# GpSimd instead of VectorE multiplies the one-hot rows of c with the three weight parts

## The chip, the cores and the metric

The kernel runs on one core of a Trainium2 chip. The core has a matrix engine (PE, TensorE), a vector engine (DVE, VectorE), an activation engine (ACT, ScalarE), a general engine (POOL, GpSimd) and a queue that issues transfers (SP, SyncE). Each engine works through its own list of instructions in order; semaphores make one engine wait for another. The metric is the device time of one execution in microseconds (us), taken as the median of several runs.

## The reference

The input is x of shape 2 x 4096 x 256, in f32. First comes a token mixer made of cumulative sums over phases, gates and a projection; it is added to x after a layer norm. Its result goes through a layer norm into a mixture of single-vector experts, and this is the part that the change is in:

```python
s1 = jnp.einsum('bshd,nd->bshn', q1, K1)      # 8 heads, 64 keys on either side
s2 = jnp.einsum('bshd,nd->bshn', q2, K2)
v1, i1 = jax.lax.top_k(s1, TOPK)              # TOPK = 10
v2, i2 = jax.lax.top_k(s2, TOPK)
all_scores = (v1[..., :, None] + v2[..., None, :]).reshape(B, S, N_HEADS, TOPK * TOPK)
all_indices = (i1[..., :, None] * N_SQRT + i2[..., None, :]).reshape(B, S, N_HEADS, TOPK * TOPK)
vals, best = jax.lax.top_k(all_scores, TOPK)
expert_idx = jnp.take_along_axis(all_indices, best, axis=-1)
scores = jax.nn.softmax(vals, axis=-1)
h = jnp.einsum('bsd,bshkd->bshk', x, W_down[expert_idx])
h = jax.nn.gelu(h, approximate=False) * scores
out = jnp.einsum('bshk,bshkd->bsd', h, W_up[expert_idx])
```

Every token picks 8 x 10 = 80 experts. Their index is i1 * 64 + i2, so only the first 4096 of the 16384 experts can be picked.

## The kernel before

The tokens are worked through in 32 blocks of 256 (16 stretches of the sequence, two batch rows each). A block passes through these stages:

- `attention` is the token mixer; it makes `xt`, `x2T` (the normed input of the experts, transposed) and the queries.
- `routes` and `route` find the 80 experts of each token. This is long work on VectorE in small instructions (MAX8, FIND_INDEX8, MATCH_REPLACE8), then one-hot sums in the tile `hot`, then the softmax `sm`. GpSimd splits `sm` into three bf16 parts which together carry the f32 value (four instructions for each half block: two casts, two subtractions, into `pk` and `rest`). TensorE transposes them, and ScalarE copies them out as `row` and `rows`: then a partition is one of the 80 picks, and the free axis is the token.
- `hidden` multiplies the block with the down vectors of all 4096 experts (weights `wd`), and ScalarE applies gelu. The result `A` has expert j (128 of them) on the partitions, and c (32) and the tokens on the free axes. Expert number = j * 32 + c.
- `weigh` (lines 935 to 989) multiplies `A` with the router's weights. For each token TensorE makes a 128 x 32 matrix of weights, as the product of a one-hot matrix over j and a one-hot matrix over c that is multiplied with the weight. The inner function `build(t0)` makes these for 32 tokens at once: `hj`, eight comparisons of 128 x 512 on VectorE; `hc`, one comparison of 128 x 1024; and `hw`, the product of `hc` with the three weight parts, 128 x 3072 in bf16 (lines 959 to 964). Then for each token TensorE loads `hj` as weights and streams the three parts of `hw` into `ps_s`, 16 tokens to a PSUM tile. VectorE multiplies each such tile into `A`.
- `outputs` multiplies `A` with the up vectors (weights `wu`), norms, adds `xt` and stores.

`weigh` runs twice for each block, and `build` four times in each: 32 x 2 x 4 = 256 builds. `build` for the next 32 tokens is called ahead of the matrix products of the current ones. The tiles `hj`, `hc` and `hw` have two buffers each, `ps_s` has two, `row` and `rows` have three.

No engine call is issued where it is written. The class `Flow` records each call as a node with its dependencies. `plan` then orders all nodes by a list schedule: it gives each call a cost (`cost`, lines 166 to 196), keeps the time at which each engine is free, and lets each engine take the ready node with the lowest number. The number is the place at which the node was recorded; `together` interleaves three streams for that (experts of this block, routes of the next, attention of the one after it). `emit` writes the order out, with semaphore waits. So nearly all instructions carry line 404 in the profile, and are told apart by their tiles; the bare weight loads carry line 403, and the matrix products that use them line 401. The cost that `plan` takes for a call depends on the engine:

```python
            elif op in ("tensor_tensor", "tensor_mul", "tensor_add", "tensor_sub") and small:
                speed = 2
            return n / speed / 0.96 + 68, n / speed / 0.96 + 160
        ...
        return n * 2.4 + 200, n * 2.4 + 400          # gpsimd
```

A call that goes to another engine therefore changes the order in which all engines do their work, and not only the place of that one call.

Of the kernel before, what the change touches and what calls it, by code (L numbers as in the profile page):

```python
# [415 lines left out]
def layer_kernel(  # L416
# [9 lines left out]
    fl = Flow(nc, tc, ctx)  # L426
# [508 lines left out]
    def weigh(A, rows, before):  # L935

        row, rows = rows
        xj = fl.tile([P, 16, P], BF16, "xj")  # L940
        fl.vector.tensor_copy(xj[:, 0, :], row)
        for s in (8, 4, 2, 1):
            v = xj.rearrange("r (a b s) t -> r a b s t", b=2, s=s)
            fl.vector.tensor_scalar(v[:, :, 1, 0, :], v[:, :, 0, 0, :], 8.0 * s, None, ALU.subtract)

        yield 3

        def build(t0):
            hj = fl.tile([P, JE, TS], BF16, "hj")
            for i in range(8):  # L950
                fl.vector.tensor_scalar(hj.rearrange("r (m j) t -> r m j t", j=8)[:, :, i, :],
                                        xj[:, :, t0 : t0 + TS], float(i), None, ALU.is_equal)
            hc = fl.tile([P, TS, EC], BF16, "hc")
            fl.vector.tensor_tensor(
                hc.rearrange("r t (a u) -> r t a u", u=RUN),
                cols.rearrange("r (a u) -> r a u", u=RUN).unsqueeze(1).to_broadcast([P, TS, EC // RUN, RUN]),
                rows[:, t0 // TS, 0].unsqueeze(2).to_broadcast([P, TS, EC // RUN, RUN]), ALU.is_equal,
            )
            hw = fl.tile([P, 3, TS, EC], BF16, "hw")
            fl.vector.tensor_mul(  # L960
                hw.rearrange("r n t (a u) -> r n t a u", u=RUN),
                hc.rearrange("r t (a u) -> r t a u", u=RUN).unsqueeze(1).to_broadcast([P, 3, TS, EC // RUN, RUN]),
                rows[:, t0 // TS, 1:4].unsqueeze(3).to_broadcast([P, 3, TS, EC // RUN, RUN]),
            )
            return hj, hw

        ready = build(0)
        yield 3
        for t0 in range(0, P, TS):
            hj, hw = ready  # L970
            if t0 + TS < P:
                ready = build(t0 + TS)
                yield 3
            for g in range(0, TS, TG):
                ps = fl.tile([P, TG, EC], F32, "ps_s")
                for t in range(0, TG, TU):
                    with fl.group():
                        for i in range(t, t + TU):
                            w = hj[:, :, g + i]
                            fl.tensor.ld(ps[:, i, :], w)  # L980
                            for n in range(3):
                                fl.tensor.mm(ps[:, i, :], w, hw[:, n, g + i, :], start=n == 0, stop=n == 2)
                    next(before, None)
                a = A[:, :, t0 + g : t0 + g + TG]
                fl.vector.tensor_mul(a, ps.rearrange("p t c -> p c t"), a)
                yield 1
        for _ in before:
            pass
        yield 1
# [90 lines left out]
```

## Time and profile before

| | |
|---|---|
| median of 3 runs | 4083.58 us (4077.91 to 4088.07) |
| the profiled execution's own time | 4087.09 us |
| span of the profiled execution | 4085.3 us |
| mean granted clock of TensorE | 0.929 |
| busy: PE, DVE, ACT, POOL | 94%, 91%, 45%, 4% |
| instructions on POOL | 264, of which 256 are the splits of the softmax |
| `hw` products on DVE | 256, mean 1742 ns, 446.0 us in all |

A row of instructions gives the line, the engine, the operation, the tiles as out<-in, the shape and type of out and in, the count after the x, the time in which at least one of them was busy, the mean duration of one in ns, and the idle time of the engine just ahead of them with what ended it. The table of stretches gives for each stretch the microseconds in which each engine was busy, with the number of instructions that began in it. The timeline gives the start, the duration, the engine and the instruction. Consecutive instructions of DVE overlap in these records by some 80 ns: the record of one ends after the next one's has begun.

### The profile page before, as it was taken

How to read it: one execution, taken by the hardware profiler on the slowest of the kernel's cores; microseconds unless marked ns; L12 is line 12 of the kernel's file. 1: busy time of each engine (PE TensorE's matmuls, PEld its weight loads, DVE VectorE, ACT ScalarE, POOL GpSimd, SP SyncE). 2: the span in 40 equal slices, each digit the busy share in tenths (PEclk: the TensorE clock that was granted, in tenths of full speed). 3: DMA queues.
4: the chain of work that ended last, by engine and by line, in shares of the span. 5: the costliest groups of instructions: out<-in, count | busy, mean ns of one | idle time of the engine just before them, and what ended most of it. 6: DMA issues, size and time to landing. Idle time of an engine off the chain costs nothing.

```text
span 4085.3 us, 79868 instructions
## 1 busy us (share of the span) xinstructions
PE 3834.6 (94%) x36870; PEld 3300.2 (81%) x20486; DVE 3735.9 (91%) x17525; ACT 1837.9 (45%) x3251; POOL 153.9 (4%) x264
## 2 busy tenths in 40 slices
PE   3499999999999999999999999999999999999998
PEld 2388888888888888888888888888888888888887
DVE  3879999999999999999999999999999999999986
ACT  3344544444544444544444544444544444544431
POOL 0000000000000000000000000000000000000000
PEclk8699999999999999999999999999999999999989
DMA  5023333223333233333233333233333233333233
GB/s 205 29 93 120 106 115 123 90 96 127 101 116 125 89 100 124 106 115 123 91 96 127 100 117 125 89 100 124 98 122 122 90 98 126 103 115 125 86 108 121
DMA packets 145151, 447.83 MB, mean 110 GB/s; under 512 B 17777, under 2 KB 44146, under 8 KB 143730
## 3 DMA queue, kind: packets, MB, share of 16 engines
q1 hardware_dynamic: 139392, 440.46, 33.2%
q8 instruction: 225, 3.69, 0.4%
q10 hardware_dynamic: 5362, 2.28, 0.2%
q14 instruction: 172, 1.41, 0.1%
HBM read 425.90 MB, written 16.78 MB: 108 GB/s over the span
## 4 chain that ended last, share of the span: by engine, by line
PE 66%; DVE 31%; ACT 2%; ACTq 1%; issue 1%; DMA 0%; POOL 0%; POOLq 0%; SPq 0%
PE ps_mm L404 35%; PE ps_s L401 16%; PE ps_acc L404 12%; DVE hj L404 6%; DVE hw L404 4%; DVE hot L404 4%; PE ps_sc L404 3%; DVE ph L404 2%; DVE A L404 2%; DVE st L404 1%; DVE iu L404 1%; DVE hc L404 1%; DVE bl L404 1%; DVE v L404 1%; ACT rows L404 1%; DVE bu L404 1%
## 5 line engine op out<-in xcount | busy, mean ns | idle before, releaser
L404 PE MATMUL ps_mm<-x2T,wd 128*128 128x256 f32 x4096 | 1115.9, 423 | 44.2 <-ACT A L404 25.8
L403 PEld LDWEIGHTS <-hj 128*128 128x128 bf16 x8192 | 963.9, 141 | 103.2 <-DVE hw L404 29.0
L404 PEld LDWEIGHTS ps_mm<-x2T,wd 128*128 128x128 f32 x4096 | 854.0, 213 | 214.0 <-issue 81.9
L401 PE MATMUL ps_s<-hw,hj 128*128 128x32 bf16 x24576 | 994.9, 189 | 31.5 <-DVE hj L404 13.8
L404 PE MATMUL ps_acc<-wu,A 128*128 128x256 f32 x4096 | 1006.6, 393 | 6.9 <-DVE o L404 4.2
L404 PEld LDWEIGHTS ps_acc<-wu,A 128*128 128x128 f32 x4096 | 792.4, 197 | 123.5 <-DVE o L404 10.2
L404 ACT ACT_TABLE_LOAD x658 | 844.2, 1283 | 38.8 <-issue 26.0
L404 ACT ACTIVATE A<-ps_mm 128x256 f32<-128x256 f32 x1024 | 349.5, 383 | 976.3 <-PE ps_mm L404 961.3
L404 DVE TENSOR_SCALAR hj<-xj 128x512 bf16<-128x512 bf16 x2048 | 512.0, 302 | 0.0
L404 DVE TENSOR_TENSOR hw<-hc,rows 128x3072 bf16<-128x3072 bf16 x256 | 446.0, 1742 | 0.0
L404 DVE TENSOR_TENSOR A<-ps_s,A 128x512 f32<-128x512 f32 x512 | 346.7, 680 | 102.3 <-PE ps_s L401 62.4
L404 DVE FIND_INDEX8 iu<-v,s 128x8 uint32<-128x64 f32 x2048 | 428.1, 217 | 0.0
L404 DVE MAX8 v<-s 128x8 f32<-128x64 f32 x2048 | 374.3, 210 | 15.9 <-ACT s L404 15.9
L404 ACT ACTIVATE sm<-sm 128x80 f32<-128x80 f32 x64 | 17.3, 270 | 706.7 <-DVE sm L404 706.6
L404 DVE MATCH_REPLACE8 s<-v,s 128x64 f32<-128x64 f32 x1024 | 210.5, 208 | 0.0
L404 POOL CAST pk<-sm 128x80 bf16<-128x80 f32 x64 | 35.6, 556 | 3830.3 <-DVE sm L404 3830.3
L404 DVE TENSOR_TENSOR hc<-cols,rows 128x1024 bf16<-128x1024 bf16 x256 | 171.1, 678 | 0.0
L404 DVE MATCH_VALUE_LOAD iu<-v,s 128x8 f32 x2048 | 149.3, 73 | 0.0
L404 DVE RECIPROCAL rs<-rs 128x2 f32<-128x2 f32 (+1 forms) x160 | 22.3, 154 | 136.5 <-ACT rs L404 136.5
L404 PE MATMUL ps_mm<-x2T,wq 128*128 128x256 f32 x512 | 125.2, 388 | 1.0 <-ACT qT L404 0.6
L404 PE MATMUL ps_sc<-kbd,qT 128*128 128x256 f32 x512 | 124.8, 386 | 0.2 <-ACT qT L404 0.2
L404 PE MATMUL ps_mm<-xT,wg 128*128 128x256 f32 x512 | 122.3, 386 | 0.3 <-ACT tmp L404 0.3
(161 smaller groups left out, 4159.7 us busy)
## 6 DMA issues: line engine op xcount, KB each, us to landing
wu<-wu_d SPq DMA_DIRECT2D x512, 512.0 KB, 4.2
wd<-wd_d SPq DMA_DIRECT2D x256, 512.0 KB, 3.5
xt<-in_attn_x_dram SPq DMA_DIRECT2D x32, 256.0 KB, 2.9
A<-in_table_dram SPq DMA_DIRECT2D x8, 1024.0 KB, 7.2
out_dram<-o SPq DMA_DIRECT2D x64, 128.0 KB, 3.1
ph<-in_attn_pos_phases_dram SPq DMA_DIRECT2D x16, 256.0 KB, 3.9
wu_d<-A SPq DMA_DIRECT2D x8, 512.0 KB, 5.2
wd_d<-wd SPq DMA_DIRECT2D x8, 512.0 KB, 3.3
```

Of the source, the lines that this page charges most:

```text
L401: return engine.add_instruction(ins)
L403: return engine.ldweights(args[1], is_transpose=kw.get("is_transpose"), tile_position=(0, 0))
L404: return getattr(engine, op)(*args, **kw)
```

## The change

The product `hw` is issued on GpSimd; operands, shapes, types and buffers stay as they are.

```diff
             hw = fl.tile([P, 3, TS, EC], BF16, "hw")
-            fl.vector.tensor_mul(
+            fl.gpsimd.tensor_mul(
                 hw.rearrange("r n t (a u) -> r n t a u", u=RUN),
                 hc.rearrange("r t (a u) -> r t a u", u=RUN).unsqueeze(1).to_broadcast([P, 3, TS, EC // RUN, RUN]),
                 rows[:, t0 // TS, 1:4].unsqueeze(3).to_broadcast([P, 3, TS, EC // RUN, RUN]),
             )
```

## The prediction

> **What bounds the kernel now.** I read the page's first part, the chain of waits and the groups, and then a table of stretches over one block.
>
> ```profile
> PE 3834.6 (94%) x36870; PEld 3300.2 (81%) x20486; DVE 3735.9 (91%) x17525; ACT 1837.9 (45%) x3251; POOL 153.9 (4%) x264
> ...
> PE 66%; DVE 31%; ACT 2%; ACTq 1%; issue 1%; DMA 0%; POOL 0%; POOLq 0%; SPq 0%
> ...
> L404 DVE TENSOR_TENSOR hw<-hc,rows 128x3072 bf16<-128x3072 bf16 x256 | 446.0, 1742 | 0.0
> ```
>
> Two engines are nearly full, PE and DVE. The chain runs through PE for two thirds and through DVE for one third. POOL is all but idle. The moved product is 446.0 of DVE's 3735.9 us, so taken alone the change frees 12% of an engine that carries a third of the chain. In the stretches (span; busy us of PE, PEld, DVE, ACT, POOL with counts; clock; DMA share; GB/s) there are two kinds:
>
> ```profile
> 1931.00:2004.00 73.00, 70.07 (x868) 61.90 (x419) 70.98 (x310) 34.81 (x57) 2.47 (x4) 0.95 0.30 96
> 2004.00:2054.00 50.00, 48.32 (x285) 40.02 (x221) 46.65 (x241) 23.70 (x48) 2.27 (x4) 0.93 0.39 128
> ```
>
> All eight `hw` of a block start in the 73 us kind (the stretch has 8 of them, 13.61 us); the 50 us kind has none. PE and DVE are above 93% in both. So nothing waits idly for DVE time to come free, and nothing on DVE may get longer without the span getting longer.
>
> **What the profile says of POOL beside DVE.** POOL's own rows, by form:
>
> ```profile
> L404 POOL TENSOR_TENSOR rest<-sm,pk 128x80 f32<-128x80 f32 x64 | 31.6, 494 | 5.1
> L453 POOL IOTA iota<- 128x108 bf16 x1 | 0.3, 345 | 0.0
> masks.py:197 POOL MEMSET ident<- 128x128 f32 x1 | 0.2, 205 | 0.3 <-POOLq L1068 0.3
> L451 POOL IOTA cols<- 128x32 bf16 x1 | 0.2, 163 | 0.0
> ```
>
> And the places in the timeline where POOL's short instructions meet DVE's:
>
> ```profile
> 187.33 0.44 POOL L404 TENSOR_TENSOR rest<-sm,pk 128x80 f32<-128x80 f32 x1
> 187.45 0.38 DVE L404 TENSOR_TENSOR hot<-hot 128x80 uint16<-128x80 uint16 x1
> ...
> 1929.26 0.65 POOL L404 CAST pk<-rest 128x80 bf16<-128x80 f32 x1
> ...
> 1929.42 0.54 DVE L404 CAST pk<-ej 128x160 bf16<-128x160 uint16 x1
> ...
> 1998.10 0.19 DVE L404 CAST pk<-ej 128x160 bf16<-128x160 uint16 x1
> ...
> 1999.47 0.72 POOL L404 CAST pk<-rest 128x80 bf16<-128x80 f32 x1
> ...
> 1999.68 0.65 DVE L404 TENSOR_SCALAR hj<-xj 128x512 bf16<-128x512 bf16 x1
> ...
> 3962.28 0.68 POOL L404 TENSOR_TENSOR pk<-rest,pk 128x80 bf16<-128x80 f32 x1
> ...
> 3962.46 0.88 DVE L404 TENSOR_TENSOR hc<-cols,rows 128x1024 bf16<-128x1024 bf16 x1
> ```
>
> The same CAST takes 0.19 us alone and 0.54 us where it starts inside a POOL instruction: POOL's ends at 1929.91, the CAST's at 1929.96. An `hj` (median 282 ns) takes 0.65 us and ends at 2000.33, 0.15 us after POOL's. So a copy, cast or tensor-scalar on DVE, SBUF to SBUF, stands still until POOL's instruction is nearly over (about 0.1 us before its recorded end). Instructions with two SBUF inputs do so too: the `hot` sum (186 ns mean) took 0.38 us, `hc` (678 ns) took 0.88 us, until POOL had done its reading. DVE works in order, so what is queued behind the standing instruction stands as well. Rows with one SBUF input pass freely: 60 `st<-xt` statistics beside POOL kept their 0.41 us.
>
> How soon after a POOL start does DVE reach such a row? An example of its queue:
>
> ```profile
> 1959.98 0.08 DVE L404 MATCH_VALUE_LOAD s<-v,s 128x8 f32 x1
> ...
> 1960.51 0.67 DVE L404 TENSOR_TENSOR A<-ps_s,A 128x512 f32<-128x512 f32 x1
> ...
> 1961.31 0.07 DVE L404 MATCH_VALUE_LOAD s<-v,s 128x8 f32 x1
> 1961.36 0.21 DVE L404 MATCH_REPLACE8 s<-v,s 128x64 f32<-128x64 f32 x1
> 1961.49 0.28 DVE L404 TENSOR_SCALAR hj<-xj 128x512 bf16<-128x512 bf16 x1
> ```
>
> Here 1.5 us of free rows (top-10 search, product out of PSUM) come ahead of an `hj`. Over the whole trace, without `hw`, DVE's work by its pitch is 3310 us: 690 us copies, casts and tensor-scalars, 980 us two SBUF inputs, 1640 us free. The free rows come in 1999 runs of 0.82 us on average; from a point taken at random it is 0.94 us to the next row that can be held.
>
> **The change part by part.**
>
> (1) Removed from DVE: 256 `hw`. One starts at 2002.60 and the next instruction at 2004.24, so each is worth 1.65 us of pitch: -425 us.
>
> (2) Added to POOL: 256 products of 3072 elements with two inputs. No row of before has this size. Lower end: MEMSET costs (205 - 100) / 127 = 0.83 ns an element (100 ns is a one-element MEMSET here), which gives 2.5 us, 2.7 us with a fixed part. Upper end: all of the 494 ns of the 80-element product but 100 ns is per element, 4.9 ns, which gives 15 us. The one row pair that shows the pace of an element loop is IOTA: (345 - 163) / 76 = 2.39 ns. With it 191 ns of the 494 are elements and 303 ns fixed, and the product takes 3072 x 2.39 + 303 = 7.6 us. I take 7.6: at 80 elements a one-input CAST (556 ns) costs no less than the two-input product, so the fixed part must be large there, and the upper end is far too high. POOL then has 256 x 7.6 = 1950 us of work, under half the span, 61 us out of each block.
>
> The Trainium skill, GPSIMD Engine Reference, section Performance versus the Vector engine, puts a two-input tensor_tensor at about 2.6 cycles an element at 1.2 GHz, and says that elementwise work belongs on VectorE. By that the product is estimated at 7.0 us, and the sum below at 5,090 us instead of 5,240.
>
> (3) What it does to DVE: each product stops DVE from the first row that can be held, 0.94 us on average after its start, to 0.1 us before its end: 7.6 - 0.94 - 0.1 = 6.56 us, times 256 = +1680 us. Ends: none at all (0), if a long instruction lets DVE in between its reads; and 256 x 14 = 3580 us at 15 us each.
>
> The Trainium skill, SBUF — State Buffer, section Who interferes with whom, says the same as these rows: VectorE and GpSimd share one pair of ports, whoever starts first keeps it for the whole instruction. It tells of no piecewise release; no run here shows an instruction of several us.
>
> (4) Idle time of DVE: 349 us now, of which 68 lie in the first 100 us, 21 in the next, 57 in the last 285. The 203 us between are mostly waits for PE and ACT (`A` for `ps_s` 62 us, `rs` for ACT 137 us). PE has 250 us idle now and gets over 1000 us, so I take half of them off: -100 us (ends: 0 and -200).
>
> (5) `hw` arrives 7.6 - 1.7 = 5.9 us later, and PE's products and DVE's `A` wait for it. The extra lies inside the time for which DVE stands in (3), so nothing is added. If it lay beside it, once for each `weigh`: 64 x 5.9 = 378 us.
>
> (6) POOL's queue is in order. The four split instructions of `route` now stand behind one or two `hw` (8 to 15 us), and an `hw` can stand behind a split that waits for `sm`. `rows` of the first half are ready 51 us ahead of their use, those of the second some 42 us (copied at 1932, first used by the product at 1974.7). That covers it: 0. Without cover it is up to 64 x 15 = 960 us.
>
> (7) The schedule is made anew on all engines: other orders of `wd`, `wu` and store issues on SP, 598 instead of 658 table loads on ACT. DMA is at 33%, ACT at 45%: 0 for both.
>
> Sum: 4087 (the profiled execution) - 425 + 1680 - 100 = 5242 us; the median of the runs lies 3.5 us lower, so 5240.
>
> **Rivals.**
>
> A. As above, both kinds of DVE rows held: 5,240. With products from 6 to 9 us, 4,830 to 5,600 (256 us for each us).
>
> B. Only the copies, casts and tensor-scalars are held; two-input rows get in, since POOL's long reading leaves gaps. For: the two-input cases here are few, and 30 of the `hot` sums beside a POOL CAST kept 0.18 us. Against: the 0.38 and 0.88 us above. Laying a 7.6 us hold behind each `hc` over DVE's rows gives 1250 us of standing instead of 1680: 4,810.
>
> C. POOL's product is much slower than 7.6 us (its operands repeat in three nested steps, and both are bf16): 10 to 12 us give 5,850 to 6,370. For: upper end of (2). Against: the IOTA pace.
>
> D. The other side: the long product takes the ports element by element and DVE hardly stands. Place: `hw` itself. Then DVE has 3310 us of work and PE is the bound with 3835 us busy plus ramp and tail, about 3,980. It decides from where the standing falls below 425 us, 1.65 us for each product; that is also the time of a 2.7 us product, the lower end of (2). Against: every row of before in which a tensor-scalar met POOL stood to POOL's end.
>
> E. DVE hardly stands but (5) or (6) is open: 4,100 to 4,500.
>
> **Chances and range.** A 0.66, B 0.13, C 0.08, D 0.08, E 0.05. Leaving out D, half of E and the far end of C, the range is 4,500 to 5,750. Slower 0.90; faster by over 0.3% 0.08; within 0.3% 0.02 (0.3% is about what a measurement of this kernel can tell from no change).
>
> **What would show it.** (2): `hw` rows on POOL, 256, mean near 7600 ns, POOL busy near 50%. (3): `hj`, `hc` and other two-input rows on DVE with means far above 282 and 678 ns, single ones of several us that end with a POOL `hw`; MAX8 and FIND_INDEX8 unchanged; DVE's busy share still above 90%, PE's down to some 73%. (4): waits of DVE for `ps_s` not above 62 us by much. (6): `rows` not late for the products. The prediction is wrong if `hj` keeps about 300 ns beside a running `hw` (then D or E), if only `hj`-like rows grow (B), or if a POOL product is far from 7.6 us.

## The result

The changed kernel takes 4766.71 us (median of 4 runs, 4764.88 to 4769.25), the kernel before 4081.25 us in the same comparison (4 runs). The ratio is 1.168, with an interval of 1.166 to 1.170: 17% slower. The profiled execution took 4767.72 us, its span is 4765.9 us.

The page of the changed kernel, its first part, the chain by engine, and the groups that answer to those shown of before:

```profile
PE 3936.5 (83%) x36870; PEld 3359.3 (70%) x20486; DVE 4444.8 (93%) x17269; ACT 1778.1 (37%) x3191; POOL 1576.6 (33%) x520
...
DVE 72%; PE 25%; ACT 2%; ACTq 0%; issue 0%; DMA 0%; POOL 0%; POOLq 0%; SPq 0%
...
L404 POOL TENSOR_TENSOR hw<-hc,rows 128x3072 bf16<-128x3072 bf16 x256 | 1421.7, 5554 | 2639.4 <-DVE hc L404 1850.4
...
L404 DVE TENSOR_SCALAR hj<-xj 128x512 bf16<-128x512 bf16 x2048 | 731.4, 409 | 0.0
L404 DVE TENSOR_TENSOR hc<-cols,rows 128x1024 bf16<-128x1024 bf16 x256 | 241.7, 945 | 6.0 <-POOL hw L404 5.3
```

The rows of `hj`, `hc` and `sm` before:

```profile
L404 DVE TENSOR_SCALAR hj<-xj 128x512 bf16<-128x512 bf16 x2048 | 512.0, 302 | 0.0
L404 DVE TENSOR_TENSOR hc<-cols,rows 128x1024 bf16<-128x1024 bf16 x256 | 171.1, 678 | 0.0
...
L404 DVE TENSOR_TENSOR sm<-bv 128x80 f32<-128x80 f32 x64 | 14.5, 226 | 0.0
```

VectorE gave away 446 us of work and is busy for 709 us longer. The chain changed sides: PE had 66% and VectorE 31% of it, now VectorE has 72%. POOL itself is on it with 0%. Its product ends one wait of VectorE, of 5.3 us, and none of PE, and it is idle for 2639 us ahead of its products. The loss sits in VectorE's other rows: `hj` went from 302 to 409 ns on average, `hc` from 678 to 945 ns.

The means hide how this happens. The view by tile gives minimum, median and maximum of the durations (ns):

```profile
L404 POOL TENSOR_TENSOR hw<-hc,rows x256: 5411/5428/7009, 172.8 to 4727.4; 128x3072 bf16<-128x3072 bf16 x128
...
L404 DVE TENSOR_SCALAR hj<-xj x2048: 244/281/5515, 187.7 to 4734.1; 128x512 bf16<-128x512 bf16 x187
...
L404 DVE TENSOR_TENSOR hc<-cols,rows x256: 659/679/5245, 172.1 to 4726.2; 128x1024 bf16<-128x1024 bf16 x128
```

The medians of `hj` and `hc` are within 1 ns of those before (282 and 678 ns). A few rows are longer by as much as a whole product of 5.43 us. In the timeline (start, duration):

```profile
2008.60 5.41 POOL L404 TENSOR_TENSOR hw<-hc,rows 128x3072 bf16<-128x3072 bf16 x1 [3.81 <-DVE hc L404]
...
2009.91 0.06 DVE L404 MATCH_VALUE_LOAD bu<-bv,cv 128x8 f32 x1
2009.97 0.17 DVE L404 FIND_INDEX8 bu<-bv,cv 128x8 uint32<-128x27 f32 x1
2010.07 4.04 DVE L404 TENSOR_TENSOR sm<-bv 128x80 f32<-128x80 f32 x1
2014.03 0.30 DVE L404 CAST bf<-bu 128x64 bf16<-128x64 uint32 x1
```

The product runs from 2008.60 to 2014.01. VectorE's search rows and one row out of PSUM pass beside it at their old durations for 1.5 us (the last two are shown). Then comes `sm`, 80 elements with two SBUF inputs, 226 ns before: it takes 4.04 us and ends at 2014.11, 0.10 us after the product. Everything behind it on VectorE stands as long.

"Standing" is the time by which VectorE's rows are longer than the median of the same row before, summed over the copies, casts, tensor-scalars and rows with two SBUF inputs. Counted so over the trace, VectorE's copies, casts and tensor-scalars are longer by 761 us in all, rows with two SBUF inputs by 438 us, and all others by -13 us. The first two make 1199 us of standing, against 58 us in the kernel before, where the softmax splits caused it. Of the 256 products 254 hold a row; the first one is reached 0.83 us after the product's start on average, and 4.6 us of standing follow. VectorE's work shrank by 432 us, its standing grew by 1141 us, which makes the 709 us; its idle time fell from 349 to 321 us. 709 - 28 = 681 us, and the span grew by 680.6.

### The profile page after: what moved, and what is told of

Same layout as the page of the kernel before. It is cut to its first block, busy times and chain, and to the rows that moved or that the text cites. A ratio compares the mean times of both kernels' runs of the same rounds, so it can differ in the third digit from the quotient of the medians.

```text
span 4765.9 us, 79988 instructions
## 1 busy us (share of the span) xinstructions
PE 3936.5 (83%) x36870; PEld 3359.3 (70%) x20486; DVE 4444.8 (93%) x17269; ACT 1778.1 (37%) x3191; POOL 1576.6 (33%) x520
## 4 chain that ended last, share of the span: by engine, by line
DVE 72%; PE 25%; ACT 2%; ACTq 0%; issue 0%; DMA 0%; POOL 0%; POOLq 0%; SPq 0%
PE ps_mm L404 13%; DVE hj L404 12%; PE ps_s L401 6%; DVE tmp L404 6%; DVE iu L404 5%; DVE hot L404 5%; PE ps_acc L404 4%; DVE hc L404 4%; DVE bl L404 4%; DVE A L404 4%; DVE xj L404 3%; DVE v L404 3%; DVE ph L404 3%; DVE sm L404 3%; DVE s L404 3%; DVE cv L404 2%
## 5 line engine op out<-in xcount | busy, mean ns | idle before, releaser
L404 POOL TENSOR_TENSOR hw<-hc,rows 128x3072 bf16<-128x3072 bf16 x256 | 1421.7, 5554 | 2639.4 <-DVE hc L404 1850.4
L404 PE MATMUL ps_mm<-x2T,wd 128*128 128x256 f32 x4096 | 1045.7, 406 | 255.1 <-DVE ph L404 139.1
L404 PE MATMUL ps_acc<-wu,A 128*128 128x256 f32 x4096 | 1147.6, 431 | 51.1 <-DVE o L404 32.5
L404 PEld LDWEIGHTS ps_acc<-wu,A 128*128 128x128 f32 x4096 | 868.0, 218 | 203.0 <-DVE o L404 44.2
L404 DVE TENSOR_SCALAR hj<-xj 128x512 bf16<-128x512 bf16 x2048 | 731.4, 409 | 0.0
L404 DVE TENSOR_TENSOR hc<-cols,rows 128x1024 bf16<-128x1024 bf16 x256 | 241.7, 945 | 6.0 <-POOL hw L404 5.3
L404 DVE TENSOR_SCALAR xn<-xt,mv,rs 128x256 f32<-128x256 f32 x128 | 201.2, 1610 | 3.0 <-PE ps_mm L404 2.9
L404 DVE TENSOR_SCALAR xj<-xj 128x128 bf16<-128x128 bf16 (+3 forms) x256 | 192.8, 753 | 0.1
L404 DVE TENSOR_SCALAR tmp<-tmp 128x512 f32<-128x512 f32 x48 | 145.3, 3027 | 6.9 <-ACT tmp L404 6.5
L404 PE MATMUL ps_mm<-xT,wg 128*128 128x256 f32 x512 | 150.6, 422 | 0.3 <-ACT tmp L404 0.3
```

The costliest lines, as they stand in the source:

```text
L404: return getattr(engine, op)(*args, **kw)
```

## The experiments

The theory, *standing*: a GpSimd instruction that reads SBUF keeps ports that VectorE's copies, casts, tensor-scalars and two-input rows need, to its end. The rivals: *lateness* (the product comes later and the engines wait for it), *total time* (the cost goes with GpSimd's busy time, whatever VectorE does meanwhile), and *order* (the planner, which sees another engine and cost, makes a worse order).

The runs together; "work" is VectorE's busy time without its standing, standing is counted as above, idle is the span less VectorE's busy time (these three are read from the profiled execution, and the time is the median of all):

| run | time us | ratio to before (interval) | work | standing | idle |
|---|---|---|---|---|---|
| before, profiled | 4087 | | 3678 | 58 | 349 |
| changed kernel | 4767 | 1.168 (1.166 to 1.170) | 3246 | 1199 | 321 |
| no product | 3765 | 0.925 (0.923 to 0.926) | 3256 | 37 | 458 |
| no product, varied tile | 3766 | 0.924 (0.922 to 0.926) | 3260 | 32 | 471 |
| twin on POOL | 4451 | 1.095 (1.091 to 1.099) | 3666 | 508 | 275 |
| blank on POOL | 4175 | 1.025 (1.022 to 1.027) | 3671 | 113 | 390 |
| three pieces | 4583 | 1.125 (1.123 to 1.127) | 3243 | 1031 | 318 |
| measured cost | 4625 | 1.134 (1.131 to 1.137) | 3247 | 1015 | 360 |
| cost 12 us | 4902 | 1.202 (1.199 to 1.204) | 3286 | 1022 | 596 |
| order control | 4065 | 0.996 (0.995 to 0.997) | 3670 | 66 | 328 |

(Run to run, the kernel before lay between 4067 and 4094 us.)

### The product left out: what VectorE's time is worth

```diff
-            hw = fl.tile([P, 3, TS, EC], BF16, "hw")
-            fl.vector.tensor_mul(hw..., hc..., rows...)
+            hw = hw_c                  # one tile, written once
```

(The two buffers of `hw` go as well, and with them PE's waits for it, 12.6 us before.)

> The product hw is left out: the matrix products read a constant tile in its place, so the weights are not the reference's. It asks what VectorE's 425 us of work are worth with nothing put on GpSimd. If PE is then the bound: PE busy 3835 us and about 150 us of ramp and tail, 3,980 us. If VectorE's part of the chain (31%) goes in full, it can't fall below PE's 3,835 us plus the ramp, some 3,900. If the work on VectorE was covered, it stays at 4,080.

Measured: 3765.03 us, lower than any of the three. Its page:

```profile
PE 3617.5 (96%) x36870; PEld 3185.6 (85%) x20486; DVE 3293.0 (88%) x17270; ACT 1859.9 (50%) x3267; POOL 200.7 (5%) x264
```

PE is the bound, as expected, but its own busy time fell by 217 us with the same 36870 instructions. The mean granted clock is 0.978 in place of 0.929. By the profile's clock records TensorE spent 581 us of the kernel before at half clock, and 169 us here. 412 us less at half pace are an estimated 206 us of PE's work, near the 217. What brings the half clock about is shown only in part. In this table of stretches of the kernel before (busy us of PE, PEld, DVE, ACT, POOL; granted clock), and in PE's timeline beside it, the clock is full up to 2010.80 and then at half until 2017.63:

```profile
2006.00:2010.00 4.00, 3.83 (x66) 3.30 (x26) 4.00 (x26) 0.19 (x1) 0.00 (x0) 1.00 0.02 4
2010.00:2014.00 4.00, 3.16 (x45) 2.46 (x17) 4.00 (x13) 0.66 (x2) 0.00 (x0) 0.60 0.12 18
2014.00:2018.00 4.00, 4.00 (x12) 3.15 (x11) 2.84 (x23) 0.67 (x3) 0.00 (x0) 0.55 0.31 113
```

```profile
2007.74 3.90 PE L401 MATMUL ps_s<-hw,hj 128*128 128x32 bf16 x96 [0.17 <-DVE A L404]
2011.48 1.20 PE L404 MATMUL ps_mm<-x2T,wd 128*128 128x256 f32 x2
2013.52 7.45 PE L404 MATMUL ps_mm<-x2T,wd 128*128 128x256 f32 x24 [0.84 <-ACT A L404]
```

PE's wait of 0.84 us comes at 2012.68, behind the fall of the clock; ahead of the fall stand the small `ps_s` products. The clock records of this trace come in steps of 3.41 us, counted here at full clock and after 200 us. Of the 110 falls, 61 follow a step that `ps_s` fills to 95% or more (there are 66 such steps), 48 one of the rest in which PE waits for over 0.1 us in all (of 145), and 1 any other (of 789). Without the product there are 16 falls behind 32 steps full of `ps_s` and 1 behind 47 steps with waits. So both kinds are rarer there; why there are fewer such `ps_s` steps, and fewer falls behind them, isn't shown.

The constant tile could have been another cause, so it was replaced by varied data:

```diff
-    fl.vector.memset(hw_c, 0.01)
+    fl.vector.tensor_copy(hw_c, cols.unsqueeze(1).unsqueeze(1).to_broadcast([P, 3, TS, EC]))
```

> As the run without the product, but the tile that the matrix products read in hw's place holds the numbers 0 to 31 and not one constant; the product is left out, the weights are not the reference's. That run had TensorE at half clock for 169 us, against 581 us in the kernel before. If TensorE's half-clock stretches come from its waits, nothing changes: within 0.5% of 3,765 us and the granted clock near 0.978. If the constant data had raised the clock, it goes back to 0.93 and the time to some 3,960 us.

Measured: 3766.04 us at a clock of 0.974. So it isn't that the data are constant. 425 us less work on VectorE are worth 310 us: in the profiled executions PE's idle time falls by 118 us and its own busy time by 217 us, the second with the clock.

### A twin on POOL: standing without lateness

```diff
             fl.vector.tensor_mul(hw..., hc..., rows...)
+            twin = fl.tile([P, 2, 832], BF16, "twin")
+            twice = hc.rearrange("r t c -> r (t c)")[:, 0:832].unsqueeze(1).to_broadcast([P, 2, 832])
+            fl.gpsimd.tensor_mul(twin, twice, twice)
```

> hw stays on VectorE; GpSimd gets an extra product of 1664 elements with two SBUF inputs (hc times hc into a scratch tile that nobody reads) for each build. Nothing waits for its result. By the measured pace (5.43 us for 3072 elements, some 0.3 us of it fixed) one takes 3.1 us. Theory of standing (VectorE stands from the first row that shares ports, 0.9 us after the start, to the end): 256 x 2.2 = +560 us, 4,640 us, with hj, scans and hc single rows of 2 to 3 us. Theory of lateness (the cost of the change is that hw comes later and the order is another): within 1% of 4,081 us.

Measured: 4451.08 us, +376 us, with nobody waiting for the result. VectorE stands 450 us more than before, 89 of them in `hw` rows. Lateness can't give this, and it is more than an order alone was seen to bring (below). Standing gives less than the 560 us that I expected. In the timeline (twin, then VectorE):

```profile
2382.72 2.96 POOL L404 TENSOR_TENSOR twin<-hc 128x1664 bf16<-128x1664 bf16 x1
...
2382.78 0.68 DVE L404 TENSOR_TENSOR A<-ps_s,A 128x512 f32<-128x512 f32 x1
2383.39 2.58 DVE L404 TENSOR_SCALAR tmp<-tmp 128x512 f32<-128x512 f32 x1
2385.89 0.15 DVE L404 RECIPROCAL rs<-rs 128x1 f32<-128x1 f32 x1
```

A tensor-scalar that took 0.42 us takes 2.58 and ends 0.29 us after the twin; the product out of PSUM ahead of it passes unhurt at 0.68. The smaller sum has two reasons in the rows: the first held row comes 1.58 us after a twin's start, not 0.83, and 20 twins hold none. And the twin stands too: it often starts right behind `hc`, close to VectorE's own `hw`. The 129 twins that meet an `hw` have a median of 4.60 us, the others of 2.96.

### A blank on POOL: writing alone

```diff
             fl.vector.tensor_mul(hw..., hc..., rows...)
+            blank = fl.tile([P, 1664], BF16, "blank")
+            fl.gpsimd.iota(blank, pattern=[[0, 52], [1, 32]], base=0, channel_multiplier=0,
+                           allow_small_or_imprecise_dtypes=True, after=[hc])
```

(`after` is a further argument of the recording layer: the call waits for `hc` without reading it.)

> hw stays on VectorE; for each build GpSimd gets an IOTA of 1664 elements into a scratch tile that nobody reads: it writes and reads nothing. By the pace of the small IOTA rows (2.39 ns an element) one takes 4.1 us. If a GpSimd instruction holds every sharing row of VectorE whatever it does itself: 256 x 3.2 = +820 us, 4,900 us. If without reads it holds only the copies, casts and tensor-scalars, and rows with two SBUF inputs pass: some +500 us, 4,580 us, with hj rows of 3 to 4 us and hc, scans and hot at their old durations. If only reading holds anything: 4,081 us.

Measured: 4175.07 us, +100 us. The size of the IOTA was misjudged, 1.77 us instead of 4.1, so the sums don't apply; but the rows tell the three cases apart. Two places in the timeline:

```profile
2155.61 1.77 POOL L405 IOTA blank<- 128x1664 bf16 x1 [31.98 <-DVE hc L405]
...
2155.66 1.73 DVE L405 TENSOR_TENSOR hw<-hc,rows 128x3072 bf16<-128x3072 bf16 x1
...
2233.99 1.92 POOL L405 IOTA blank<- 128x1664 bf16 x1 [7.07 <-DVE hc L405]
...
2233.84 2.22 DVE L405 TENSOR_SCALAR xn<-xt,mv,rs 128x256 f32<-128x256 f32 x2
```

A product with two SBUF inputs runs all along beside the IOTA and takes its usual 1.73 us. Two `xn` tensor-scalars, 0.73 us together when free, take 2.22. Over the trace, 157 two-input rows and 632 others began inside an IOTA at least 0.4 us before its end, and none grew by more than 0.3 us; all 30 copies, casts and tensor-scalars that did so stood, by 1.49 us on average. So a GpSimd instruction that only writes holds only the second kind, the middle case. The Trainium skill, SBUF — State Buffer, section Who interferes with whom, says this very thing: two SBUF inputs contend with a GpSimd instruction that reads SBUF and not with one that only writes. VectorE's standing rose by 55 us here, its idle time by 41. Where the idle time comes from wasn't tried; it is of the size that another order brings (below).

### Three pieces, and one piece

```diff
-            fl.gpsimd.tensor_mul(hw..., hc..., rows[:, t0 // TS, 1:4]...)
+            for n in range(3):
+                fl.gpsimd.tensor_mul(hw[:, n]..., hc..., rows[:, t0 // TS, 1 + n]...)
```

> hw on GpSimd as in the changed kernel, but as three products of 1024 elements, one for each weight part, one after the other. One takes 0.3 + 1024 x 1.67 ns = 2.0 us, three 6.0 us. If VectorE gets through between two GpSimd instructions, and again runs 0.9 us before it has to stand: 768 x 1.1 = 845 us of standing instead of 1155, 4,460 us. If standing goes by GpSimd's total time (the next piece starts before VectorE gets on): 256 x 5.1 = 1305 us, 4,910 us.

Measured: 4582.54 us, 184 us less than the changed kernel. Standing fell from 1199 to 1031 us although GpSimd's busy time rose from 1577 to 1713 us, and the time is 327 us below what *total time* asked for, more than an order alone was seen to bring: it falls as a theory. The 184 us themselves can't be put down to the pieces, since the order is new here as well, and another order of the uncut product gained 142 us (below). That VectorE gets in between two pieces is read from the rows. The gain is smaller than expected since VectorE gets only one held row through between two pieces and then meets the next one soon:

```profile
2004.59 1.64 DVE L404 TENSOR_TENSOR sm<-bv 128x80 f32<-128x80 f32 x1
2006.15 2.03 DVE L404 CAST bf<-bu 128x64 bf16<-128x64 uint32 x1
2007.98 0.45 DVE L404 TENSOR_SCALAR xj<-xj 128x1024 bf16<-128x1024 bf16 x1
```

The three pieces run from 2002.26 to 2008.01 here: `sm` gets in after the second, `bf` waits for the end of the third.

```diff
-            fl.vector.tensor_mul(hw..., hc..., rows[:, t0 // TS, 1:4]...)
+            fl.gpsimd.tensor_mul(hw[:, 0]..., hc..., rows[:, t0 // TS, 1]...)
+            fl.vector.tensor_mul(hw[:, 1:3]..., hc..., rows[:, t0 // TS, 2:4]...)
```

> Of the three weight parts, GpSimd multiplies one (1024 elements) and VectorE two (2048). VectorE gets rid of a third of hw's work, 256 x 0.53 = -137 us. Theory of standing: a GpSimd product of 1024 elements took 2.08 us in the three pieces, and VectorE stood 1.27 us for each (975 us for 768), so +325 us, and the sum is 4,075 - 137 + 325 = 4,265 us. If what counts is how late hw comes, a product of 2 us is hardly later than VectorE's 1.7 us, and the time is 4,075 us or less.

Measured: 4191.27 us, ratio 1.027 (1.024 to 1.029): slower than before by 113 us, less than the 188 expected, and not faster, as lateness would have it. With the whole product on GpSimd an order alone was seen to bring as much (below), so the time by itself doesn't decide. But VectorE is busy for 56 us longer (3792 us) though a third of `hw` has left it, and idle for 49 us longer. Groups of this run:

```profile
L404 DVE TENSOR_TENSOR hw<-hc,rows 128x2048 bf16<-128x2048 bf16 x256 | 386.0, 1508 | 0.0
...
L404 POOL TENSOR_TENSOR hw<-hc,rows 128x1024 bf16<-128x1024 bf16 x256 | 676.7, 2644 | 2836.7 <-DVE hc L404 2210.9 <-PE ps_s L401 586.7 <-DVE v L404 32.3
```

VectorE's two parts have a minimum of 1.18 us and a mean of 1.51, POOL's one part 1.93 and 2.64: both products start behind the same `hc` and hold each other. POOL's turn often falls into VectorE's product, where it is POOL that stands. VectorE's standing rises by 104 us and its `hw` rows are 83 us over their minimum, together some 0.7 us for each POOL product, not the 1.27 expected.

### The order

```diff
-        return n * 2.4 + 200, n * 2.4 + 400      # the planner's cost of a GpSimd call
+        return n * 1.67 + 300, n * 1.67 + 300
```

In the changed kernel:

> The changed kernel, where the planner takes for GpSimd what was measured (1.67 ns an element and 300 ns: 5.43 us for hw) instead of 7.57 us. Theory of standing: the order shifts, VectorE's work and standing do not, so within 1.5% of 4,767 us. If the loss came from an order made for a wrong duration, it falls clearly, below 4,650 us.

Measured: 4625.11 us, 142 us less than the changed kernel: beyond the 1.5% I allowed, and just inside what I had set for the rival. The rows say how it does it. VectorE's work is the same 3247 us, its standing 1015 us in place of 1199, its idle time 39 us more. The first held row comes 1.11 us after a product's start, not 0.83, and 33 products hold no row where 2 did. So the order acts through the standing; but I was wrong to think that it would leave it as it was. A fifth of the change's loss of 686 us hung on this one order. A cost of 12 us:

```diff
-        return n * 2.4 + 200, n * 2.4 + 400
+        return n * 3.8 + 300, n * 3.8 + 300
```

> The changed kernel with a planner's cost of 12 us for hw (3.8 ns an element and 300 ns) in place of 7.57. Theory of standing: VectorE's own work is unchanged and the time is its work (3,250 us), its standing and some 320 us of idle time; the order sets only how soon after a product's start VectorE meets a row that is held, so between 4,600 and 5,000 us, and the time follows the standing counted in the rows. If a plan that reserves more time for the product were the cure, it falls below 4,400 us.

Measured: 4902.07 us. Standing is 1022 us, as little as with the measured cost, and yet the time is 277 us higher. It doesn't follow the standing alone:

```profile
PE 3986.7 (81%) x36870; PEld 3388.1 (69%) x20486; DVE 4307.9 (88%) x17269; ACT 1798.4 (37%) x3206; POOL 1549.1 (32%) x520
```

VectorE is idle for 596 us. Its waits are for PE and ACT, spread over many places:

```profile
DVE rs L404 <- ACT rs L404: 103.6, 47, 22.7
DVE rsd L404 <- PE ps_mm L404: 82.6, 18, 5.2
DVE v L404 <- ACT s L404: 67.1, 32, 12.5
...
DVE ph L404 <- PE ps_mm L404: 54.7, 18, 5.8
DVE bl L404 <- PE ps_mm L404: 49.7, 32, 13.4
```

Only the plan differs, so the plan makes these waits; how it does so wasn't followed up. The control, the same first edit in the kernel before, where it touches only the plan for the four small splits:

> The kernel before, all work where it was; only the planner's cost for GpSimd is the smaller one (1.67 ns an element and 300 ns), which concerns the four splits alone. It shows what another order by itself does when no work moves. If the +0.7% of the run with the splits off GpSimd was such an effect, this one moves by 0.3% to 1.5% in either direction. If orders of this kind are all worth the same, 4,078 us within 0.3%.

Measured: 4065.29 us, ratio 0.996 (0.995 to 0.997). With no work moved, the order alone is worth 0.4% here. It is the only kernel of this study with the whole computation that is faster than the kernel before.

### Less beside VectorE, and less on it

```diff
-        fl.gpsimd.tensor_copy(parts[0], sm)
-        fl.gpsimd.tensor_sub(rest, sm, parts[0])
-        fl.gpsimd.tensor_copy(parts[1], rest)
-        fl.gpsimd.tensor_sub(parts[2], rest, parts[1])
+        fl.scalar.copy(parts[0], sm)
+        fl.vector.tensor_sub(rest, sm, parts[0])
+        fl.scalar.copy(parts[1], rest)
+        fl.vector.tensor_sub(parts[2], rest, parts[1])
```

> The kernel before, where the four split instructions of the softmax leave GpSimd: the two casts go to ScalarE, the two subtractions to VectorE. GpSimd then does nothing beside VectorE. Theory of standing: 59 us of VectorE's rows standing for the splits go (123 rows longer by over 0.3 us), 128 small subtractions of some 0.15 us come (+19 us), so -40 us, 4,035 us, and no hj or pk cast is longer than about 0.3 us. If such standing doesn't reach the end, 4,075 us. If the chain through three engines comes late for rows: 4,100 us or more.

Measured: 4107.88 us, ratio 1.007 (1.005 to 1.010). The rows did what the theory said: no row of VectorE is longer than its old median by over 0.3 us, where 123 were, and the `pk` cast went from 355 to 183 ns. The time did not follow. One term was mis-sized: the 128 subtractions that VectorE got were to cost 19 us, and their rows show 53:

```profile
L404 DVE TENSOR_TENSOR pk<-rest,pk 128x80 bf16<-128x80 f32 x64 | 33.4, 523 | 0.8
...
L404 DVE TENSOR_TENSOR rest<-sm,pk 128x80 f32<-128x80 f32 x64 | 19.3, 302 | 0.4
```

So VectorE's busy time fell by 9 us only, and its idle time rose by 28 us. Of its waits one grew and one shrank:

```profile
DVE A L404 <- PE ps_s L401: 155.8, 92, 28.1
DVE rs L404 <- ACT rs L404: 57.7, 35, 21.9
```

`A` waited 62 us for `ps_s` before, and `rs` 137 us for ScalarE. The order was made anew here too, and 0.7% is not far from the 0.4% that an order alone made in the control. Whether the new order or the longer chain over three engines made the idle time stays open.

```diff
-            fl.vector.tensor_scalar(xn[:, j, :], xt[:, j, :], mv[:, j, 0:1], rs[:, j : j + 1], ALU.subtract, ALU.mult)
+            fl.scalar.activation(xn[:, j, :], xt[:, j, :], AF.Identity, scale=rs[:, j : j + 1], bias=nb[:, j : j + 1])
...
```

> As the run with the splits off GpSimd, and the 256 normalising instructions of the layer norms (xn, y, the second xn, o) on ScalarE, with scale and bias; VectorE makes the bias with one small instruction for each norm. VectorE loses about 92 us by pitch and gets about 13 us. If VectorE's work carries the time at the rate that leaving hw out showed (310 us for 425 us), -58 us more than the run with the splits alone: 3,980 us. ScalarE has the room (45% busy) and gets 256 x 0.38 = +97 us. If ScalarE's order delays the attention chain: no better than the run with the splits alone.

Measured: 4139.26 us, ratio 1.014 (1.012 to 1.016): the rival. VectorE's busy time fell by 82 us, and its idle time rose from 349 to 471 us. PE now waits for ScalarE's norm where it waited for VectorE's:

```profile
PE ps_mm L404 <- ACT xn L404: 122.8, 31, 7.0
```

That was 38 us with `xn` on VectorE.

## Why the prediction was right, and where it was off

The sign, the mechanism and the range held: rival A, 17% slower, inside 4,500 to 5,750. The point, 5,240, was too high by 473 us, and one of the prediction's own signs of being wrong came true: a POOL product far from 7.6 us. The range was wide enough for it. By its steps:

1. 425 us removed from VectorE: right. Its work without standing fell by 432 us.
2. 7.6 us for the product: the mis-sized term. It took 5.43 us (median). Two sizes give the pace: minimum 1.93 us for 1024 elements and 5.41 us for 3072, so 1.70 ns an element and 0.19 us fixed. The IOTA pair that I took for the pace of an element loop (2.39 ns) doesn't even hold for IOTA: 1664 elements took 1.77 us. 2.17 us too much, 256 times, is 556 us, more than the whole error. The Trainium skill, GPSIMD Engine Reference, section Performance versus the Vector engine, gives some 2.6 cycles an element for two inputs (f32); 1.70 ns at its 1.2 GHz are 2.0 cycles for this bf16 product. The measurement decides.
3. Standing from 0.94 us after the start to 0.1 us before the end: right. Measured 0.83 us to the first held row and 4.6 us of standing. With the product's real 5.43 us the step gives 256 x 4.39 = 1124 us, against 1141 measured.
4. Idle time of VectorE -100 us: measured -28. PE has 829 us of idle time, not over 1000, and its busy time, taken as fixed, grew by 102 us at a mean clock of 0.869 in place of 0.929.
5. and 6. Lateness and POOL's queue at nothing: held. VectorE waited 54 us for `ps_s` (62 before), and `hc` 0.7 us for `rows`. PE waited 12.6 us for `hw` before and never for it after.
7. The new order at nothing: a gap. Two other orders of the same instructions gave 4625 and 4902 us, so it can carry -3% to +3%, through standing as well as through idle time. No run moved the product and kept the order of before, so how much of the 686 us belongs to the changed kernel's order stays open.

With steps 2 and 4 as measured: 4087 - 425 + 1124 - 28 = 4758 us, against 4768 for the profiled execution. That it comes so near is luck in part: for the run with the measured cost, step 3 gives the same 1124 us, where 957 us were measured.

Rival B (only copies held) is refuted by the 438 us in two-input rows. Its best support, 30 `hot` sums that kept 0.18 us beside a POOL CAST, isn't explained by any run here. D's mechanism is refuted by the rows, and its floor of 3,980 us was wrong too: without the product the kernel runs in 3,765 us, because PE's own time isn't fixed: it was 217 us shorter.

## What to carry to other kernels

GpSimd's idle time isn't free room beside a busy VectorE: price an offload by VectorE's standing, the GpSimd duration less the stretch until VectorE reaches a copy, a cast, a tensor-scalar or a two-input SBUF row, and look for such standing in the small GpSimd instructions that the profile already has (here 58 us of it, and the one try to remove it didn't pay). In this kernel no size tried, from 1024 to 3072 elements, paid. And where a planner remakes the order with every edit, a few tenths of a per cent up to some per cent belong to the order: run a control that changes only the plan before a small gain or loss is put down to the edit.

## What the runs showed of the hardware that I had not expected

- PE's busy time moves with the granted clock, and the clock falls without long waits too: 581 us at half clock before, 1255 in the changed kernel, 169 without the product. The Trainium skill, TensorE: Matmul & The Clock Gate, section HAM oscillation — how this bites in real kernels, warns of idle gaps beyond some 3.4 us. In the kernel before, 61 of 110 falls came right behind 3.41 us filled with `ps_s` products, and where a fall followed a wait, PE had waited for 1.0 us (median) of the 3.41. The records show no wait inside a run of `ps_s`, but the ends of matrix products are modelled in them.
- GpSimd is held as well: a 2.96 us product had a median of 4.60 us where it met VectorE's `hw`, and one of 1.93 us, issued behind the same `hc` as a VectorE product, a mean of 2.64 us.
- A GpSimd IOTA of 1664 elements took 1.77 us, about as long as VectorE's product of 3072 (1.74 us).
